# A ring of value tiles in another part of memory, eighteen stores on another queue, and a new order for the first of two phases

## The chip, the core and the metric

The kernel runs on one core of a Trainium2 chip. Five engines work side by side: TensorE (PE; the loads of its stationary operand are shown apart as PEld), VectorE (DVE), ScalarE (ACT), GpSimd (POOL) and SyncE (SP), which here does nothing but issue transfers (DMAs) between the chip's DRAM and the on-chip SBUF. [...] The metric is the device time of one execution in microseconds (us), taken as the median of several runs.

## What is computed

A decoder layer in float32 over 32 batches of 128 rows of 512 values: causal self-attention with rotary positions, cross-attention to a context, and a feed-forward block with ternary weights. A residual and a layer norm follow each. Cut to what matters:

```python
def self_attention(x):                      # x [32, 128, 512], 16 heads of 32
    q, k, v = heads(x @ Wq.T), heads(x @ Wk.T), heads(x @ Wv.T)
    q, k = rope(q), rope(k)
    s = where(causal, q @ k.T / sqrt(32), -inf)
    return merge(softmax(s) @ v) @ Wo.T

def cross_attention(x, ctx):                # 8 heads of 16: a head is 16 of the 128 ROWS
    q, k, v = (t.reshape(32, 8, 16, 512) for t in (x, ctx, ctx))
    s = einsum('bhdq,bhdl->bhql', q, k) / sqrt(16)      # 512 x 512 for each head
    return gamma * einsum('bhql,bhdl->bhdq', softmax(s), v).reshape(32, 128, 512)

def bitlinear(x, w, b):                     # int8 activations, weights of -1, 0 and 1
    return act_quant(rms_norm(x)) @ weight_quant(w).T + b

def ffn(x):                                 # 512 -> 2048 -> 512
    h = gelu(silu(bitlinear(x, w1, b1)))
    return bitlinear(layer_norm(h, g, b), w2, b2)

x = ln(x + self_attention(x))
x = ln(x + cross_attention(x, ctx))
out = ln(x + ffn(x))
```

## The kernel before

**Two phases.** Phase 1 (L255 to L591) does the self-attention of all 32 batches and leaves its results in DRAM. Phase 2 (L594 to the end) does cross-attention and the feed-forward block of all 32 batches from there. The *seam* below is the stretch in which the last batches of phase 1 (batch 31 is the last) and the first of phase 2 meet.

**Phase 1, a batch.** `load` fetches x as it is and transposed. `project` (L338 to L348) multiplies by a weight of 512 columns. Both operands are split into a high and a low part, which gives 12 matmuls of 128x512 in three steps of four; a step is one unit for the planner. A batch has four projections: queries and keys (*side* 0 and 1 of `rope`), values, and the output projection `wo`. `rope` turns queries and keys by products on DVE (L407 to L410) and sums on POOL (L414, L415). `stage_s` transposes both (L430, tile `banka`, copied by DVE to `qkT`) and computes the scores of 16 heads in four groups that the code calls heads 0 to 3 (L447). The softmax of a group goes mask and row maximum on DVE (L459), exponential on ACT (L465), reciprocal and product on DVE or POOL, four transposes on PE (L477) and a copy (L480, tile `prT`). `stage_o` weighs the values (L496), projects, and normalises on POOL (L514 to L519) into `x1`, which is stored in DRAM as `x1d` (L521).

**The parts.** `split3` (L350 to L365) turns a float32 tile into three bfloat16 parts: a cast on ACT, a difference on POOL (tile `spr`), a cast on ACT, a difference on POOL. All three lie in a tile `sp`. Six DMAs of 128 KB then store parts 0, 1, 2, 0, 1, 0 one after the other as `qd` (L364). `context` does the same with the context: six stores as `kd`, with the parts in another order, and the values times gamma as `cd`. With 96 rows of such parts (six pairs of 16 rows) one bfloat16 matmul of phase 2 gives nearly a float32 product. `quantize_weights` prepares the ternary weights in between.

**Phase 2, half a batch (four heads).** `kp` and `qp` are tiles of 98 rows x 4 heads x 512: 96 rows of parts, and two rows that shift the scores by their maximum. In `kp` these are ones (from the DRAM tile `ones_d`), in `qp` the negated maxima, in a high and a low part (tiles `mhi`, `mlo`). The work goes: 16 times scores `mx` on PE (L677) and a maximum on DVE (L681); a transpose, and two rows of maxima (L694, L695) stored into `qp` by two SP DMAs (L700); then 16 scores `sT` on PE with all 98 rows (L756), 16 exponentials `ex` on ACT (L759) and 16 matmuls with the values, `acc` (L766). The values lie in a ring of three tiles `cT` of 128 x 32 x 32 float32: half of each tile is loaded from `cd` (L663), the other half is ones, set once (L616), so that the same matmul gives the sum of the exponentials. Softmax division, layer norm and feed-forward block follow.

**Who sets the order.** Nothing is written down in the order in which it runs. `Plan` (L83 to L217) is a list scheduler that runs while the program is built. Every operation has a kind ("PE.qkv", "SP.xs"), a cost in us, and a priority: its batch number plus the offset of its kind in a table, `OFF1` for phase 1 and `OFF2` for phase 2. At each step the planner takes, among the first open operation of every kind, the one that can start in the earliest time slot, and in one slot the one of lowest priority. Each engine then runs its instructions in exactly the planned order, and so a changed offset or cost reorders engines and queues and nothing else. A DMA is one operation of "SP" with a cost for its issue and a latency until it has landed.

**The seam in the code.** When the last projection of queries, keys and values ("PE.qkv") has been planned, the planner calls `early` (L578). It releases the projection weights, which lie at the right end of SBUF, and opens a pool "qk" there with four `kp` and four `qp` tiles. Twelve SP DMAs fill them for the first two batches of phase 2: for each tile pair a ones row, the key parts, the query parts. These twelve stand in the middle of SP's queue, among the stores of the last batches of phase 1. The tiles of phase 2 proper, the `cT` ring among them, come from pools opened after phase 1 on the left, where phase 1's working tiles were. So the three memsets of L616 are the first that POOL does in phase 2.

```python
        pl.op("SP." + kind, max(0.55, kb / 340), fn, ins, outs, prio, 2.2 + kb / 340, rel)
        ...
        st2.close()
        qk = pool(ctx, "qk", side="right")
        ...
    vring = [cb.tile([P, 2 * XD, NC * XH], F32, tag=f"cT{i}", name=f"cT{i}") for i in range(CFG["cT"])]
    for t in vring:
        nc.gpsimd.memset(t[:, XD:], 1.0)
```

The framework adds the waits between engines: one of a tile's later user for an earlier one, one of a newly opened pool's tile for those that used the same place, and one for each DMA completion that is needed. A DMA's completion is counted on one of a few semaphores that all DMAs of the program use in turn.

Of the kernel before, what the change touches and what calls it, by code (L numbers as in the profile page):

```python
# [11 lines left out]
F32 = mybir.dt.float32  # L12
# [11 lines left out]
P = 128  # L24
# [5 lines left out]
XH = 8  # L30
XD = S // XH
DI = 2048
NC = D // P
# [9 lines left out]
Q_PARTS = (0, 1, 2, 0, 1, 0)  # L43
# [23 lines left out]
OFF1 = {'SP.x': 76.47, 'SP.w': -83.56, 'ACT.w': 1251.46, 'DVE.wl': 97.39, 'DVE.w': 1455.82, 'SP.wq': 258.11, 'ACT.wq': -501.07, 'DVE.wq': -718.11, 'PE.wq': 497.75, 'ACT.xh': -83.03, 'Pool.xl': -493.52, 'PE.qkv': 642.06, 'DVE.rope': -749.29, 'Pool.rope': 726.68, 'ACT.v': -277.88, 'SP.cx': 161.38, 'ACT.cs': 561.27, 'Pool.cs': 151.36, 'Pool.cs3': 444.12, 'SP.cs': -169.59, 'SP.ct': -341.75, 'ACT.ct': 5.76, 'SP.cv': 657.35, 'PE.qkT': -233.53, 'DVE.qkT': -713.26, 'PE.sc': 223.31, 'DVE.mask': -673.03, 'ACT.exp': 343.93, 'DVE.rd': 481.16, 'DVE.pr': 893.48, 'PE.prT': -342.18, 'DVE.prT': 602.51, 'ACT.prT': 121.56, 'Pool.pr': 38.32, 'PE.pv': 403.29, 'ACT.oh': 297.53, 'DVE.ol': -241.16, 'PE.wo': 645.28, 'DVE.y': -873.41, 'Pool.y': 255.11, 'Pool.x1': -113.85, 'SP.x1': 730.76, 'ACT.xs': 299.8, 'Pool.xs': -1039.81, 'Pool.xs3': 582.54, 'SP.xs': 975.4}  # L67
C1 = dict(pace=15.0, xs=4, pr=5, prT=7, ra=3, qkT=4, sp=3, spr=2, xhe='ACT', lne='Pool', s1e='Pool', s2e='ACT', cxl=-0.5, wq=3.0, nb=32, wst=4, mm=3, tr=3, sc=4, scc=1.1, po=1, pc=4, spe='ACT', cte='ACT', s3e='Pool', qke='DVE', pre=['DVE', 'DVE', 'Pool', 'Pool'], prTe=['DVE', 'ACT', 'ACT', 'ACT'], wl=24.0, slack=0.02)

class Buf:  # L70

# [11 lines left out]
class Plan:  # L83
# [5 lines left out]
    slack = 0.1  # L89
# [131 lines left out]
def decoder_kernel(ctx: ExitStack, tc: tile.TileContext, x, xT, cx, cxT, wqkT, wvT, woT, gamma,  # L221
                   w1T, b1, ln_g, ln_b, w2T, b2, cst, out):
    nc = tc.nc

    def pool(stack, name, bufs=1, **kw):
        return stack.enter_context(tc.tile_pool(name=name, bufs=bufs, **kw))
# [23 lines left out]
    q_d = [dram.tile([6, XD, XH, D], BF16, tag=f"qd{b}", name=f"qd{b}") for b in range(NB)]  # L250
# [4 lines left out]
    with ExitStack() as st1:  # L255
# [6 lines left out]
        pl = Plan(nc, tc, OFF1)  # L262
        NB1 = C1['nb']

# [33 lines left out]
        def dma(kind, fn, kb, ins=(), outs=(), prio=0.0, rel=0.0):  # L298
            pl.op("SP." + kind, max(0.55, kb / 340), fn, ins, outs, prio, 2.2 + kb / 340, rel)
# [38 lines left out]
        def project(kind, pq, parts, w, sl, wb, prio):  # L338

            steps = [(a, t, c) for a, t in ((0, 0), (1, 0), (0, 1)) for c in range(NC)]  # L340
            m = C1['pc']
            for i in range(0, 12, m):
                def mm(i=i):
                    for k in range(i, i + m):
                        a, t, c = steps[k]
                        nc.tensor.matmul(pq.t, parts[a].t[:, c, :], w[t][:, c, sl], start=k == 0, stop=k == 11)  # L346
                used = [parts[0]] + ([parts[1]] if i + m > 4 else [])
                pl.op("PE." + kind, 0.236 * m, mm, used + [wb], (pq,), prio)  # L348

        def split3(kind, v, dst, parts, prio):  # L350

            sp, r = pl.buf("sp"), pl.buf("spr")
            e = C1['spe']
            pl.op(f"{e}.{kind}", 0.48 if e == "ACT" else 0.6, lambda: cp(e)(sp.t[:, 0, :], v.t), (v,), (sp,), prio)

            e1, e2 = C1['s1e'], C1['s2e']
            pl.op(f"{e1}.{kind}", 0.6 if e1 == "DVE" else 1.225, lambda: en(e1).tensor_tensor(
                r.t, v.t, sp.t[:, 0, :], ALU.subtract), (v, sp), (r,), prio)
            pl.op(f"{e2}.{kind}", 0.52 if e2 == "ACT" else 0.34, lambda: cp(e2)(sp.t[:, 1, :], r.t), (r,), (sp,), prio)  # L359
            e3 = C1['s3e']  # L360
            pl.op(f"{e3}.{kind}3", 1.0 if e3 == "DVE" else 1.2, lambda: en(e3).tensor_tensor(  # L361
                sp.t[:, 2, :], r.t, sp.t[:, 1, :], ALU.subtract), (r, sp), (sp,), prio)
            for s, k in enumerate(parts):
                dma(kind, lambda s=s, k=k: nc.sync.dma_start(dst[s].rearrange("t h c -> h t c"), sp.t[:, k, :]), 131,  # L364
                    (sp,), (), prio)  # L365

        def context(b):
            at = b
# [117 lines left out]
        def stage_o(b):  # L486
            at = b
            po, oh, ol, v = pl.buf("po"), pl.buf("oh"), pl.buf("ol"), PV[b]
# [30 lines left out]
            pl.op(e + ".x1", 0.46 if e == "DVE" else 0.76, lambda: en(e).tensor_scalar(  # L519
                x1.t, y.t, nm.t, rs.t, ALU.add, ALU.mult), (y, nm, rs), (x1,), at)  # L520
            dma("x1", lambda: nc.sync.dma_start(x1_d[b], x1.t), 262, (x1,), (), at)  # L521
            split3("xs", x1, q_d[b], Q_PARTS, at)


        def quantize_weights(k, src, dst):
# [47 lines left out]
            stage_o(b)  # L573
        pl.slack = C1['slack']
        NQ = CFG['NQ']
        kring, qring = [], []

        def early():  # L578

            st2.close()  # L580
            qk = pool(ctx, "qk", side="right")
            for i in range(NQ):
                k = qk.tile([NROW, 4, D], BF16, tag=f"kp{i}", name=f"kp{i}")
                q = qk.tile([NROW, 4, D], BF16, tag=f"qp{i}", name=f"qp{i}")
# [22 lines left out]
    for name, n, shape, dtype in (  # L607
# [2 lines left out]
            ("q1T", 2, (P, NC, P), FP16), ("z", CFG["z"], (P, DI), F32), ("q2", 2, (P, DI), FP16),  # L610
            ("q2T", CFG["q2T"], (P, NI, P), FP16), ("t1", 1, (P, D), F32)):
        pl.tag(name, n, pb, shape, dtype)

    vring = [cb.tile([P, 2 * XD, NC * XH], F32, tag=f"cT{i}", name=f"cT{i}") for i in range(CFG["cT"])]
    for t in vring:
        nc.gpsimd.memset(t[:, XD:], 1.0)  # L616
    pl.tag("cT", CFG["cT"], ring=vring)
    pl.tag("kp", NQ, ring=kring)
    pl.tag("qp", NQ, ring=qring)
# [465 lines left out]
```

## Time and profile before

| what | value |
|---|---|
| runs | 1667.03, 1671.82 and 1674.67 us; median 1671.82 |
| the profiled execution | 1675.28 us; span 1673.5 us, granted TensorE clock 0.973 |
| PE, PEld | 1551.4 us (93%), 785.0 us (47%) |
| DVE, ACT, POOL | 1383.9 us (83%), 1432.7 us (86%), 1251.5 us (75%) |
| DMA queue of the kernel | 256.78 MB, 52.8% of 16 engines' span |
| DRAM | 142.41 MB read, 92.81 MB written |
| 0 to 50 us | PE busy 33.46, ACT 22.72 |
| 600 to 700 us | PE busy 95.31 |
| 800 to 1000 us | PE 193.23, DVE 185.27, ACT 187.33, POOL 170.47 |
| 1400 to 1600 us | PE 186.23 |
| 1600 us to the end | PE 27.65 |

All times inside an execution are counted from the start of its span; the 1.8 us between span and time lie around it. Phase 1 runs until about 565 us and phase 2 from there. The costliest lines, from the groups of instructions (line, engine, operation, output tile and input tile, shapes, count; busy us and mean ns of one; idle time before them and what ended most of it):

```profile
L681 DVE TENSOR_REDUCE mt<-mx 128x1 f32<-128x512 f32 x1024 | 643.4, 679 | 54.9 <-PE mx L677 52.9
L759 ACT ACTIVATE ex<-sT 128x512 f32<-128x512 f32 x1024 | 533.9, 615 | 77.9 <-PE sT L756 74.4
L677 PE MATMUL mx<-kp,qp 96*128 96x512 bf16 x1024 | 336.9, 386 | 21.5 <-DVE mt L681 17.7
L756 PE MATMUL sT<-qp,kp 98*128 98x512 bf16 x1024 | 320.7, 385 | 15.9 <-DMA qp<-mlo 13.3
L766 PE MATMUL acc<-ex,cT 128*32 128x512 f32 x2048 | 289.4, 637 | 0.0
```

A wait is shown as the name behind "<-": the instruction or DMA whose end released the one that stood idle. A queue of SP is written "SPq", and a DMA "DMA qd<-sp" by the tiles it goes from and to.

### The profile page before, as it was taken

How to read it: one execution, taken by the hardware profiler on the slowest of the kernel's cores; microseconds unless marked ns; L12 is line 12 of the kernel's file. 1: busy time of each engine (PE TensorE's matmuls, PEld its weight loads, DVE VectorE, ACT ScalarE, POOL GpSimd, SP SyncE). 2: the span in 40 equal slices, each digit the busy share in tenths (PEclk: the TensorE clock that was granted, in tenths of full speed). 3: DMA queues.
4: the chain of work that ended last, by engine and by line, in shares of the span. 5: the costliest groups of instructions: out<-in, count | busy, mean ns of one | idle time of the engine just before them, and what ended most of it. 6: DMA issues, size and time to landing. Idle time of an engine off the chain costs nothing.

```text
span 1673.5 us, 30270 instructions
## 1 busy us (share of the span) xinstructions
PE 1551.4 (93%) x9540; PEld 785.0 (47%) x9540; DVE 1383.9 (83%) x3315; ACT 1432.7 (86%) x2950; POOL 1251.5 (75%) x1679
## 2 busy tenths in 40 slices
PE   6999999999999799999999999999999999999844
PEld 4878777777778333333333333333333333333211
DVE  6877776777777678899999989899899999998674
ACT  4889989899976367999989989899999999998963
POOL 3777778777787404679879888878978888986772
PEclk8999999999999799999999999999999999999977
DMA  6476677766664654355455345545544544544221
GB/s 226 163 236 232 226 231 244 255 233 214 209 208 153 185 177 122 93 129 145 113 133 147 105 129 139 131 115 139 142 110 128 153 110 134 149 122 123 69 62 50
DMA packets 235680, 258.71 MB, mean 155 GB/s; under 512 B 110072, under 2 KB 159224, under 8 KB 235136
## 3 DMA queue, kind: packets, MB, share of 16 engines
q1 hardware_dynamic: 235520, 256.78, 52.8%
q8 instruction: 75, 1.23, 0.3%
q14 instruction: 85, 0.70, 0.1%
HBM read 142.41 MB, written 92.81 MB: 141 GB/s over the span
## 4 chain that ended last, share of the span: by engine, by line
PE 41%; DVE 18%; POOL 16%; DMA 9%; ACT 8%; issue 7%; SPq 1%; POOLq 0%; ACTq 0%; DVEq 0%
PE banka L346 12%; DVE mt L681 8%; PE acc L766 7%; PE sT L756 6%; POOL z L972 6%; PE mx L677 5%; PE m L925 2%; DVE am L998 2%; PE banka L477 2%; DMA qd<-sp 2%; POOL z L794 2%; PE banka L447 2%; ACT pr L465 1%; ACT ex L759 1%; PE banka L496 1%
## 5 line engine op out<-in xcount | busy, mean ns | idle before, releaser
L681 DVE TENSOR_REDUCE mt<-mx 128x1 f32<-128x512 f32 x1024 | 643.4, 679 | 54.9 <-PE mx L677 52.9
L759 ACT ACTIVATE ex<-sT 128x512 f32<-128x512 f32 x1024 | 533.9, 615 | 77.9 <-PE sT L756 74.4
L677 PE MATMUL mx<-kp,qp 96*128 96x512 bf16 x1024 | 336.9, 386 | 21.5 <-DVE mt L681 17.7
L756 PE MATMUL sT<-qp,kp 98*128 98x512 bf16 x1024 | 320.7, 385 | 15.9 <-DMA qp<-mlo 13.3
L766 PE MATMUL acc<-ex,cT 128*32 128x512 f32 x2048 | 289.4, 637 | 0.0
L465 ACT ACTIVATE pr<-pr,nm 128x128 f32<-128x128 f32 x512 | 198.9, 394 | 4.1 <-DVE nm L459 4.1
L756 PEld LDWEIGHTS <-kp 98*128 98x128 bf16 x1024 | 90.3, 98 | 223.7 <-issue 125.1
L677 PEld LDWEIGHTS <-qp 96*128 96x128 bf16 x1024 | 96.3, 98 | 195.5 <-issue 95.1
L972 POOL TENSOR_TENSOR z<-z,bb_b 128x512 f32<-128x512 f32 x119 | 154.4, 1301 | 0.3
L972 POOL TENSOR_TENSOR z<-z,g_b 128x512 f32<-128x512 f32 x119 | 153.5, 1297 | 0.5
L459 DVE CUSTOM_DVE_ANT_0 pr<-banka,cmask 128x128 f32<-128x128 f32 x512 | 111.0, 286 | 35.9 <-PE banka L447 35.2
L1009 PE MATMUL m<-w2q,q2T 128*128 128x512 fp8e4 x464 | 116.7, 385 | 16.4 <-DMA q2T<-q 16.4
L766 PEld LDWEIGHTS acc<-ex,cT 128*32 128x32 f32 x2048 | 70.6, 184 | 114.1 <-issue 108.8
L925 PE MATMUL m<-w1q,q1T 128*128 128x512 fp8e4 x464 | 119.1, 378 | 2.7 <-DVE z L928 1.3
L1009 PEld LDWEIGHTS <-q2T 128*128 128x128 f16 x512 | 51.0, 101 | 104.5 <-DMA q2T<-q 34.9
L465 ACT ACTIVATION_READ_ACCUMULATOR pr<-pr,nm 128x1 f32 x512 | 98.0, 191 | 0.0
L794 POOL TENSOR_SCALAR z<-z,nmu,rs 128x512 f32<-128x512 f32 x119 | 94.5, 801 | 1.8
L361 POOL TENSOR_TENSOR sp<-spr,sp 128x512 bf16<-128x512 f32 x64 | 76.7, 1200 | 20.3 <-ACT sp L359 18.2
L928 DVE SCALAR_TENSOR_TENSOR z<-m,dq,b_b 128x512 f32<-128x512 f32 x116 | 85.0, 733 | 1.8 <-PE m L925 1.5
L925 PEld LDWEIGHTS <-q1T 128*128 128x128 f16 x512 | 49.2, 97 | 76.1 <-issue 19.9
L846 POOL TENSOR_TENSOR num<-num,rden 128x512 f32<-128x512 f32 x29 | 37.1, 1278 | 62.3 <-DMA rden<-rd 62.2
L346 PE MATMUL banka<-wqkh,xh 128*128 128x512 f32 x256 | 73.9, 411 | 10.3 <-ACT xh L388 10.3
(152 smaller groups left out, 3247.9 us busy)
## 6 DMA issues: line engine op xcount, KB each, us to landing
kd<-sp SPq DMA_DIRECT2D x192, 128.0 KB
qd<-sp SPq DMA_DIRECT2D x192, 128.0 KB
kp<-kd SPq DMA_DIRECT2D x64, 384.0 KB
qp<-qd SPq DMA_DIRECT2D x64, 384.0 KB
F<-f SPq DMA_DIRECT2D x64, 256.0 KB
xt<-in_xT SPq DMA_DIRECT2D x32, 256.0 KB
xs<-in_x SPq DMA_DIRECT2D x32, 256.0 KB
ct<-in_cxT SPq DMA_DIRECT2D x32, 256.0 KB
```

The costliest lines, as they stand in the source:

```text
L346: nc.tensor.matmul(pq.t, parts[a].t[:, c, :], w[t][:, c, sl], start=k == 0, stop=k == 11)
L459: nc.vector.tensor_tensor_reduce(pr.t[:, c, :], sc.t[:, c * P:(c + 1) * P], cmask, -1.0, 3e38, ALU.add, ALU.min, nm.t[:, c:c + 1])
L465: nc.scalar.activation(pr.t[:, c, :], pr.t[:, c, :], AF.Exp, scale=-1.0, bias=nm.t[:, c:c + 1], accum_out=den.t[:, c:c + 1])
L677: nc.tensor.matmul(sc.t[:, j, :], q.t[0:NPR, h, (qc + j) * P:(qc + j + 1) * P], k.t[0:NPR, h, :], start=True, stop=True)
L681: pl.op("DVE.mx", 0.064 + 0.534 * W, lambda: nc.vector.tensor_reduce(mt.t[:, i:i + W], sc.t, AX.X, ALU.max), (sc,), (mt,), p, join=True)
L756: nc.tensor.matmul(sc.t[:, i, :], k.t[:, h, lc * P:(lc + 1) * P], q.t[:, h, :], start=True, stop=True)
L759: pl.op("ACT.ex", 0.052 + 0.426 * SW, lambda: nc.scalar.activation(ex.t[:, j:j + SW, :], sc.t, AF.Exp, scale=1.0 / XD ** 0.5), (sc,), (ex, ...
L766: nc.tensor.matmul(acc.t[32 * h:32 * h + 32, :], v.t[:, :, XH * lc + 4 * g + h], exs[h // 2].t[:, h % 2, :], start=lc == 0, stop=lc == NC - 1)
L794: pl.op(e + "." + p, cost + 0.1, lambda: en(e).tensor_scalar(o.t[:, sl], v.t[:, sl], sh.t, sc.t, ALU.add, ALU.mult), ins, outs, prio)
L925: nc.tensor.matmul(flat(pz)[:, i * 512:(i + 1) * 512], q1T.t[:, c, :], w1q[:, c, (n + i) * 512:(n + i + 1) * 512], start=c == 0, stop=c == ...
L972: pl.op(e + kind, 0.148 + 0.0021 * w if e == "Pool" else 0.05 + 0.00105 * w, lambda: en(e).tensor_tensor(t(), t(), other[:, sl], op), src, ...
L1009: nc.tensor.matmul(flat(py)[:, 0:D], q2T.t[:, c, :], w2q[:, c, :], start=c == 0, stop=c == NI - 1)
```

## The change

Five edits, all of them around phase 1 and the seam. Phase 2's table `OFF2`, its settings and its code stay as they are, but for the place of the ring.

1. The table `OFF1` has new offsets for all kinds of phase 1, and one new kind, "ACT.xsd".
2. The planner's cost of a projection matmul is 0.244 us instead of 0.236.
3. `split3` has a parameter `late`. For the last three batches (29, 30 and 31) it is true for the query parts: their 18 stores are issued by ScalarE (`nc.scalar`), with a kind of their own, a cost of 0.55 and a latency of 2.6. All other stores stay on SyncE.
4. The three `cT` tiles come from the pool "qk" at the right end, ahead of the `kp` and `qp` tiles, where projection weights were.
5. Their memsets are issued in `early`, that is, in POOL's queue in the middle of phase 1's last batches, and no longer at the start of phase 2.

```diff
-OFF1 = {'SP.x': 76.47, 'SP.w': -83.56, 'ACT.w': 1251.46, ...
+OFF1 = {'SP.x': 69.66, 'SP.w': -164.57, 'ACT.w': 1533.56, ... 'ACT.xsd': 300.57}
-C1 = dict(pace=15.0, xs=4, ...
+C1 = dict(late=3, pace=15.0, xs=4, ...
...
-                pl.op("PE." + kind, 0.236 * m, mm, used + [wb], (pq,), prio)
+                pl.op("PE." + kind, 0.244 * m, mm, used + [wb], (pq,), prio)
...
-        def split3(kind, v, dst, parts, prio):
+        def split3(kind, v, dst, parts, prio, late=False):
...
             for s, k in enumerate(parts):
-                dma(kind, lambda s=s, k=k: nc.sync.dma_start(dst[s].rearrange("t h c -> h t c"), sp.t[:, k, :]), 131,
-                    (sp,), (), prio)
+                q = nc.scalar if late else nc.sync
+                pl.op("ACT.xsd" if late else "SP." + kind, 0.55, lambda s=s, k=k, q=q: q.dma_start(
+                    dst[s].rearrange("t h c -> h t c"), sp.t[:, k, :]), (sp,), (), prio, 2.6)
...
-            split3("xs", x1, q_d[b], Q_PARTS, at)
+            split3("xs", x1, q_d[b], Q_PARTS, at, b >= NB1 - C1['late'])
...
-        kring, qring = [], []
+        kring, qring, vring = [], [], []
         def early():
             st2.close()
             qk = pool(ctx, "qk", side="right")
+            for i in range(CFG["cT"]):
+                t = qk.tile([P, 2 * XD, NC * XH], F32, tag=f"cT{i}", name=f"cT{i}")
+                nc.gpsimd.memset(t[:, XD:], 1.0)
+                vring.append(t)
             for i in range(NQ):
...
-    vring = [cb.tile([P, 2 * XD, NC * XH], F32, tag=f"cT{i}", name=f"cT{i}") for i in range(CFG["cT"])]
-    for t in vring:
-        nc.gpsimd.memset(t[:, XD:], 1.0)
     pl.tag("cT", CFG["cT"], ring=vring)
```

The stores that remain on SyncE have a planned cost of 0.55 and a latency of 2.6 as well; `dma` gives 0.55 and 2.2 + 131 / 340 = 2.59 for them before.

More of the change, by code (lines that the diff above doesn't have):

```diff
@@ L66 @@
 OFF2 = {'SP.const': -264.67, 'x.kq': 390.3, 'SP.v': 77.29, 'PE.mx': -381.13, 'DVE.mx': 126.92, 'PE.mT': -632.22, 'DVE.mT': 8.23, 'SP.m': -156.28, 'PE.sT': -531.43, 'ACT.ex': -687.83, 'PE.pv': 37.38, 'ACT.acc': -737.17, 'SP.f': 49.63, 'SP.fd': 1119.71, 'SP.fn': 725.19, 'SP.fx': 343.0, 'DVE.rd': -172.57, 'SP.fr': -316.31, 'SP.fb': 17.98, 'Pool.y': -355.28, 'DVE.y': -82.99, 'Pool.yn': -277.59, 'DVE.c1': -57.25, 'Pool.c1': -358.01, 'Pool.c1m': -627.03, 'Pool.q1a': -78.8, 'Pool.x2b': 72.59, 'SP.q1T': -375.73, 'PE.c1': 39.79, 'DVE.z': -137.9, 'ACT.gelu': -406.78, 'DVE.nmu': -80.22, 'ACT.sq': -333.32, 'Pool.zn': -48.07, 'Pool.zt': 303.63, 'Pool.zb': -221.61, 'ACT.sq2': 252.58, 'DVE.am2': 91.79, 'Pool.c2': -682.87, 'Pool.c2m': -291.19, 'ACT.q2a': -262.61, 'DVE.q2a': -514.12, 'SP.q2T': 382.04, 'PE.c2': 86.97, 'DVE.c3': 17.23, 'Pool.c3': -278.83, 'Pool.c3n': 302.38, 'SP.out': 77.71, 'SP.kq': -42.69, 'DVE.yn': -735.62, 'DVE.c1m': 785.24, 'DVE.q1a': 467.22, 'DVE.zn': 550.15, 'DVE.zb': -508.13, 'DVE.c2m': -306.12, 'DVE.c3n': 99.96}
-OFF1 = {'SP.x': 76.47, 'SP.w': -83.56, 'ACT.w': 1251.46, 'DVE.wl': 97.39, 'DVE.w': 1455.82, 'SP.wq': 258.11, 'ACT.wq': -501.07, 'DVE.wq': -718.11, 'PE.wq': 497.75, 'ACT.xh': -83.03, 'Pool.xl': -493.52, 'PE.qkv': 642.06, 'DVE.rope': -749.29, 'Pool.rope': 726.68, 'ACT.v': -277.88, 'SP.cx': 161.38, 'ACT.cs': 561.27, 'Pool.cs': 151.36, 'Pool.cs3': 444.12, 'SP.cs': -169.59, 'SP.ct': -341.75, 'ACT.ct': 5.76, 'SP.cv': 657.35, 'PE.qkT': -233.53, 'DVE.qkT': -713.26, 'PE.sc': 223.31, 'DVE.mask': -673.03, 'ACT.exp': 343.93, 'DVE.rd': 481.16, 'DVE.pr': 893.48, 'PE.prT': -342.18, 'DVE.prT': 602.51, 'ACT.prT': 121.56, 'Pool.pr': 38.32, 'PE.pv': 403.29, 'ACT.oh': 297.53, 'DVE.ol': -241.16, 'PE.wo': 645.28, 'DVE.y': -873.41, 'Pool.y': 255.11, 'Pool.x1': -113.85, 'SP.x1': 730.76, 'ACT.xs': 299.8, 'Pool.xs': -1039.81, 'Pool.xs3': 582.54, 'SP.xs': 975.4}
@@ L68 @@
-C1 = dict(pace=15.0, xs=4, pr=5, prT=7, ra=3, qkT=4, sp=3, spr=2, xhe='ACT', lne='Pool', s1e='Pool', s2e='ACT', cxl=-0.5, wq=3.0, nb=32, wst=4, mm=3, tr=3, sc=4, scc=1.1, po=1, pc=4, spe='ACT', cte='ACT', s3e='Pool', qke='DVE', pre=['DVE', 'DVE', 'Pool', 'Pool'], prTe=['DVE', 'ACT', 'ACT', 'ACT'], wl=24.0, slack=0.02)
+OFF1 = {'SP.x': 69.66, 'SP.w': -164.57, 'ACT.w': 1533.56, 'DVE.wl': 224.13, 'DVE.w': 1487.99, 'SP.wq': 296.08, 'ACT.wq': -463.09, 'DVE.wq': -742.95, 'PE.wq': 461.12, 'ACT.xh': -34.87, 'Pool.xl': -579.88, 'PE.qkv': 642.47, 'DVE.rope': -636.7, 'Pool.rope': 753.46, 'ACT.v': -325.1, 'SP.cx': 56.25, 'ACT.cs': 587.4, 'Pool.cs': 196.32, 'Pool.cs3': 467.79, 'SP.cs': -292.4, 'SP.ct': -402.26, 'ACT.ct': 97.5, 'SP.cv': 685.21, 'PE.qkT': -268.05, 'DVE.qkT': -750.98, 'PE.sc': 176.14, 'DVE.mask': -511.77, 'ACT.exp': 361.28, 'DVE.rd': 495.43, 'DVE.pr': 1021.3, 'PE.prT': -437.64, 'DVE.prT': 623.36, 'ACT.prT': 100.45, 'Pool.pr': 84.22, 'PE.pv': 437.14, 'ACT.oh': 229.14, 'DVE.ol': -202.02, 'PE.wo': 645.76, 'DVE.y': -849.92, 'Pool.y': 94.83, 'Pool.x1': -7.25, 'SP.x1': 682.13, 'ACT.xs': 266.21, 'Pool.xs': -957.67, 'Pool.xs3': 476.1, 'SP.xs': 1037.25, 'ACT.xsd': 300.57}
@@ L70 @@
+C1 = dict(late=3, pace=15.0, xs=4, pr=5, prT=7, ra=3, qkT=4, sp=3, spr=2, xhe='ACT', lne='Pool', s1e='Pool', s2e='ACT', cxl=-0.5, wq=3.0, nb=32, wst=4, mm=3, tr=3, sc=4, scc=1.1, po=1, pc=4, spe='ACT', cte='ACT', s3e='Pool', qke='DVE', pre=['DVE', 'DVE', 'Pool', 'Pool'], prTe=['DVE', 'ACT', 'ACT', 'ACT'], wl=24.0, slack=0.02)
 class Buf:
```

## The prediction, made before the changed kernel was run

> **What bounds the kernel now.** I read the table by windows first, then the chain of waits around the seam between the phases, then the order in time there. The first shows who is busy in each stage (columns: stretch, its length, busy time of PE, PEld, DVE, ACT and POOL with counts, granted TensorE clock, DMA share, GB/s):
>
> ```profile
> 50.00:548.00 498.00, 488.20 (x4064) 391.45 (x4061) 366.24 (x1554) 440.38 (x1419) 381.25 (x441) 1.00 0.66 219
> 548.00:565.00 17.00, 14.14 (x93) 10.30 (x92) 10.33 (x26) 11.09 (x37) 12.49 (x17) 1.00 0.86 231
> 565.00:586.00 21.00, 12.99 (x25) 2.21 (x24) 14.61 (x26) 1.24 (x2) 5.42 (x9) 0.52 0.54 184
> 586.00:600.00 14.00, 14.00 (x69) 4.59 (x68) 9.10 (x16) 9.65 (x19) 0.00 (x0) 0.87 0.22 64
> ```
>
> Phase 1 is TensorE's: from 50 to 548 us it idles 498.00 - 488.20 = 9.8 us, so a new plan of the same work has little to win there. The seam is not TensorE's: between 565 and 586 PE is busy 13 of 21 us, at a clock of 0.52. What holds it is a chain of DMAs (start, length, what):
>
> ```profile
> 550.96 7.67 DMA qp<-qd
> ...
> 558.69 6.67 DMA qd<-sp
> ...
> 565.44 4.83 DMA qd<-sp
> ...
> 571.42 5.36 DMA x1d<-x
> ...
> 576.79 5.44 DMA qd<-sp
> ...
> 582.45 1.45 POOL cT L616 x3
> ```
>
> The last query-part store is issued at 576.79 and lands at 582.23. The value ring's memset waits for it, and so does the SyncE queue:
>
> ```profile
> 563.31 1.27 SPq L521 DMA_DIRECT2D x1d<-x  x2
> ...
> 568.86 0.77 POOL L519 TENSOR_SCALAR x<-ya,nm,rs 128x512 f32<-128x512 f32 x1 [2.81 <-DMA x1d<-x]
> ...
> 572.05 5.31 SPq L364 DMA_DIRECT2D qd<-sp  x8
> ...
> 582.37 0.33 SPq L663 DMA_DIRECT2D cT<-cd  x1
> 582.75 0.62 SPq L700 DMA_DIRECT2D qp<-mhi  x1
> 583.42 0.57 SPq L700 DMA_DIRECT2D qp<-mlo  x1
> ...
> 585.55 1.44 PE L756 MATMUL sT<-qp,kp 98*128 98x512 bf16 x3 [7.06 <-DMA qp<-mlo]
> ...
> 586.22 1.58 ACT L759 ACTIVATE ex<-sT 128x512 f32<-128x512 f32 x3 [14.06 <-PE sT L756]
> ```
>
> The value load stands in SyncE's queue with every store before it as its wait; the two row maxima (mhi, mlo), which DVE has finished by 574.87, stand behind it until 582.75. So the first exponential of phase 2 comes at 586.22. The order of every engine in phase 2 is the same in both built programs, and PE is busy 193 to 197 of every 200 us there, so what the first exponential gains or loses should reach the end.
>
> **The start of phase 1.** PE idles 3.06 us before the first transposes (15.78 to 18.84) and 2.64 us for the last value weight (24.54 to 27.18). The new order puts a 1.7 us step of the second projection into the first gap, and batch 0's second transposes ahead of the value projection. Walking it with the old rows: second projection ends at 22.9, its rotation 3.06 us later (25.96), transposes 0.4, value steps held by the same weight at 27.18, scores, last value step: 33.4 against 33.81. I take -0.4, between -3.1 (the whole gap saved) and +2 (a step of 1.9 us in front of late data).
>
> **The rest of phase 1.** The PE work is the same, instruction for instruction in number. What changes is how much of it stands between a batch's scores and the transposes of its fourth head, that is, what covers the softmax: counted in order at 0.93 us per four wide matmuls, 0.44 per four transposes, 1.10 per scores and 1.01 per weighing, 13.94 us in the mean before, 13.29 after, the least 10.2 in both. In 50 to 548 us PE waited 16 times behind the softmax, 8.5 us together, 3.2 of them so:
>
> ```profile
> PE banka L496 <- ACT prT L480: 3.2, 4, 1.8
> ```
>
> If each such wait grows by 0.65: +10.4; if all vanish: -8.5. I take +1, the middle, because nearly all heads have 12 us of cover on both sides.
>
> **The memset, moved into POOL's queue of phase 1.** Three of 0.52 us, 1.45 together, now stand behind the last projection (549.12) and before POOL's step on batch 28 (548.91). That step starts at 550.6 instead of 548.91; ACT's cast behind it stalls from 550.85 to 551.77, and the last two heads' exponentials, the last weighing and all of the tail with them: +1.0. The old place (582.45) held nobody, since the first matmul that reads cT is at 590.06: saved there, 0.
>
> **The 18 stores on ACT.** Each DMA of the program counts on one of eight semaphores, and its issue waits until the DMA before it on that semaphore has landed. By the built program's waits, the ones row of kp3 on SyncE now waits for the second store of batch 29, which ACT issues; the kp3 and qp3 loads for the third and fourth; four of batch 28's six stores for later ones of batches 29 and 30; x1d29 for the kp3 load; and batch 31's normalisation on POOL for x1d29, as before. So SyncE stands at 552 until ACT gets to its stores. Step by step, 0.58 per issue (the median of the row of these stores on SyncE, 576 ns; there is no DMA issue on ACT in this trace):
> - ACT's cast before the stores ends at 561.05 + 1.0 = 562.05; the second store starts at 562.65 and lands after 3.0, between 2.1 (the mlo row, 583.42 to 585.52, on quiet engines) and 6.67: 565.65. The old SyncE passed this place at 552.99.
> - kp3 load at 566.3, qp3 at 567.5, the six stores of batch 28 to 571.4. x1d29 needs the kp3 load: 3.5 us (the load of 549.46, landed by 552.99) to 7.67; I take 5.0: 571.4. It lands 5.5 later (563.31 to 568.86 before): 577, between 575 and 579.5.
> - Batch 31 on POOL then starts 8.1 us later than its 568.86. From there: 0.77, cast 0.62, three stores 1.74 (POOL's 1.15 beside them), cast 0.62, six more stores 3.5: the last issue starts 7.2 later (7.93 before), at 584.2.
> - It lands 4.4 later (3.0 to 5.44): 588.6, between 585 and 592.
>
> The first exponential waits for all these stores in both programs, since its pool is released as a whole: before it was free at 582.23 and the maxima came later; now the maxima come first (x1d31 at 577.8, landed 583.2, mlo behind it on its semaphore, 585.3) and the stores decide. 588.6 - 586.22 = +2.4. PE has done three score matmuls and two maxima matmuls by then; its fourth, at 587.64 before, follows the first exponential at 589.2: +1.6, between -2 and +5.
>
> Here the Trainium skill speaks against the change. The seam's share of 0.54 at 184 GB/s, with 1.00 and 332 GB/s in 600 to 605 us, leaves room for a second issuer. "DMA: Bandwidth & Descriptors", section Issuing engines are not separate DMA queues, says that issuing from more engines saves only the issuer's own time. By it the gain is at most 18 x 0.58 = 10.4 us of SyncE's queue; by the row the landing is what waits, and the sum goes by that.
>
> **The sum.** -0.4 + 1 + 1.6 (the memset is inside it) = +2.2. The profiled execution took 1675.28 us for a span of 1673.5, so 1677.5; the median of the runs, 1671.82, is 3.46 below that execution: 1674.0.
>
> **Rivals.**
> - *The seam does what it was rebuilt for.* If ACT's stores land so early that x1d29 isn't held, the last store is issued near 576 and lands near 580: 580.2 instead of 586.22, -6, with -0.4 and half of phase 1's softmax waits (-4): 1661. For it: the idle ACT (1.24 us in 565 to 586). Against: the kp3 row's wait, which a faster DMA can't move ahead of ACT's cast.
> - *An issue costs more on ACT.* Price: two stores before the kp3 row, two more before x1d29's chain, ten after batch 31 is ready, so 14 issues in line. At SyncE's slowest, 1.24 us, 14 x 0.66 = 9.2 more: 1683. It makes the kernel slower by 0.5% from 1.02 us per issue.
> - *The thinner cover bites:* +10.4 instead of +1: 1683. For it: ACT is 440 of 498 us busy. Against: the least cover is unchanged.
> - *The change does not do what it says:* the stores move but gain nothing, SyncE isn't held either, and the last store lands at 582.2 plus the memset's 1.0: the maxima no longer matter, 583.3, -3: 1668.
>
> **How the numbers follow.** The forecast has 0.52, the rivals 0.17, 0.13, 0.13 and 0.05. 0.5% is 8.4 us, about what a measurement of this kernel can tell from no change. Forecast: 0.05 faster, 0.40 the same, 0.07 slower; first rival 0.13 faster, 0.04 the same; second 0.09 slower, 0.04 the same; third 0.11 slower, 0.02 the same; last 0.02 faster, 0.02 the same, 0.01 slower. Together 0.20, 0.52, 0.28. The three terms' bounds, taken as independent, give 1674 - 10.4 and + 11.5: range 1664 to 1685, which takes in the slower rivals and leaves out most of the first.
>
> **What would show it.** Right: in the profile after, the kp<-ones_d row that was at 552.99 stands near 565; x1d<-x for batch 29 near 571; the first exponential is released by a store, within 3 us of 588.6; the last projection ends within 3 us of 549.1 and POOL's memset follows it at once. Wrong: if SyncE's queue flows through 553 to 563 as before, if ACT's issues are longer than 0.8 us, or if PE's idle time in 50 to 548 is more than 5 us off 9.8.

## The result and the profile after

The changed kernel takes 1686.52 us (median of 6 runs, 1683.19 to 1689.70), the kernel before 1670.75 us in 6 runs beside it. The ratio is 1.0071 with a 95% interval of 1.0052 to 1.0090: slower by 0.7%, some 12 us. (The two medians lie further apart, 15.8 us, but the six runs of the kernel before alone spread over 10 us; the ratio with its interval is used from here on.) The profiled execution took 1683.79 us for a span of 1682.0 us, 8.5 us longer than that before.

**Where the time goes.** First the table by windows, in the stretches shown of before (columns as there):

```profile
50.00:548.00 498.00, 482.43 (x3923) 382.35 (x3922) 355.97 (x1494) 431.76 (x1393) 368.88 (x433) 1.00 0.67 217
548.00:565.00 17.00, 16.48 (x169) 13.04 (x167) 13.86 (x52) 12.09 (x47) 10.34 (x17) 1.00 0.42 111
565.00:586.00 21.00, 16.58 (x75) 6.21 (x75) 15.39 (x28) 4.22 (x8) 9.55 (x14) 0.81 0.61 183
586.00:600.00 14.00, 4.95 (x11) 1.21 (x10) 5.00 (x9) 2.02 (x4) 3.08 (x3) 0.50 0.49 160
```

PE did 3923 matmuls in 498 us where it did 4064, and from 548 to 565 it is still at work that was over before. So phase 1 itself is longer, and the whole seam is moved back. Fixed windows can't say by how much, since the work in them differs. Equal work can. Each matmul that the trace records in phase 1 gets its usual length (0.2335 us in a projection, 0.11 in a transpose, 0.0345 in the scores and 0.0316 in the weighing, which have 32 records each in a batch); that makes 512 us. The *middle* below is the stretch from the moment 40 us of this work are done to the moment 480 are: the same 440 us of PE work in every kernel. The table by windows, with just this stretch, before and then after:

```profile
65.16:527.90 462.74, 452.94 (x3715) 362.49 (x3714) 336.52 (x1410) 413.59 (x1319) 357.77 (x416) 1.00 0.68 226
```

```profile
63.24:536.69 473.45, 458.08 (x3716) 362.95 (x3714) 335.46 (x1402) 409.30 (x1310) 350.76 (x413) 1.00 0.67 219
```

The counts agree to one matmul, and the second takes 10.7 us more at the same clock. Half of it is idle time; the other half looks like 5.1 us more busy time, because the ends of matmuls are modelled and a short wait hides in them. The waits of PE in this stretch (who waits for whom; us in total, times, longest), three before and then the same three after:

```profile
PE banka L430 <- POOL ra L415: 1.1, 3, 0.5
PE banka L496 <- ACT prT L480: 3.2, 4, 1.8
PE banka L477 <- POOL pr L470: 1.1, 4, 0.4
```

```profile
PE banka L431 <- POOL ra L416: 5.0, 7, 2.0
PE banka L497 <- ACT prT L481: 4.8, 4, 1.8
PE banka L478 <- POOL pr L471: 3.2, 7, 1.3
```

The second and third are the softmax: the weighing and the transposes of the probabilities. The first is the transposes of queries and keys, which wait for the rotation on POOL. Where the hidden half went shows when matmuls are counted from start to start: what is above their usual lengths is 22.9 us before and 33.6 after. Ahead of the weighing it grew by 5.2 us (3.7 to 8.9), ahead of the transposes of queries and keys by 4.8 (2.4 to 7.2), ahead of those of the probabilities by 0.7 (9.5 to 10.2); the rest is 7.3 us in both.

**The seam after**, in order of time:

```profile
570.99 2.52 ACTq L365 DMA_DIRECT2D qd<-sp  x3
...
574.96 0.23 SPq L593 DMA_DIRECT2D kp<-ones_d  x1
...
577.37 6.47 SPq L365 DMA_DIRECT2D qd<-sp  x6
...
583.94 0.89 SPq L522 DMA_DIRECT2D x1d<-x  x2
...
588.03 0.77 POOL L520 TENSOR_SCALAR x<-ya,nm,rs 128x512 f32<-128x512 f32 x1 [10.79 <-DMA x1d<-x]
588.83 0.32 SPq L522 DMA_DIRECT2D x1d<-x  x1
588.84 0.62 ACT L354 CAST sp<-x 128x512 bf16<-128x512 f32 x1 [14.67 <-POOL x L520]
...
590.76 4.91 ACTq L365 DMA_DIRECT2D qd<-sp  x7
...
599.22 1.09 ACT L761 ACTIVATE ex<-sT 128x512 f32<-128x512 f32 x2 [7.86 <-DMA qd<-sp]
```

The waits of SyncE's queue from 540 to 600 have this line, and before the change no such line:

```profile
SPq L593 <- DMA qd<-sp: 8.3, 1, 8.3
```

This is the chain of the prediction, link for link: the ones row of the fourth key tile (L593) waits 8.3 us for a store and stands at 574.96. In the trace it counts on the same semaphore as ScalarE's second store, issued at 572.24. SyncE's stores and the x1 stores come behind it, POOL's step on batch 31 waits 10.79 us for one of them, ACT 14.67 us for POOL, and the first exponential is released by a store. The last projection of queries, keys and values ended at 558.2 here and at 549.1 before; from there to the first exponential it takes 41.0 us and took 37.1.

### The profile page after: what moved, and what is told of

It is laid out like the page before. It is cut to its first block, busy times and chain, and to the rows that moved or that the text cites. A ratio compares the mean times of both kernels' runs of the same rounds, so it can differ in the third digit from the quotient of the medians.

```text
span 1682.0 us, 30248 instructions
## 1 busy us (share of the span) xinstructions
PE 1554.0 (92%) x9540; PEld 783.9 (47%) x9540; DVE 1386.0 (82%) x3315; ACT 1431.0 (85%) x2950; POOL 1245.9 (74%) x1679
## 4 chain that ended last, share of the span: by engine, by line
PE 37%; POOL 18%; DVE 14%; ACT 12%; DMA 9%; issue 4%; SPq 2%; ACTq 0%; POOLq 0%; DVEq 0%
PE banka L346 9%; PE acc L768 7%; DVE mt L683 6%; POOL z L974 6%; PE sT L758 6%; PE mx L679 5%; ACT pr L466 4%; PE m L927 2%; DVE am L1000 2%; PE banka L478 2%; POOL z L796 2%; DMA rden<-rd 1%; ACT ex L761 1%; DMA den<-F 1%; PE banka L448 1%
## 5 line engine op out<-in xcount | busy, mean ns | idle before, releaser
L1011 PE MATMUL m<-w2q,q2T 128*128 128x512 fp8e4 x464 | 117.6, 387 | 16.5 <-DMA q2T<-q 16.5
L848 POOL TENSOR_TENSOR num<-num,rden 128x512 f32<-128x512 f32 x29 | 37.9, 1308 | 68.2 <-DMA cT<-cd 53.2
L361 POOL TENSOR_TENSOR sp<-spr,sp 128x512 bf16<-128x512 f32 x64 | 75.8, 1188 | 14.8 <-ACT sp L359 13.9
L390 POOL TENSOR_TENSOR xl<-xt,xh 128x512 fp32r<-128x512 f32 x32 | 42.5, 1327 | 59.3 <-ACT xh L389 59.3
```

The source lines that it names most:

```text
L1011: nc.tensor.matmul(flat(py)[:, 0:D], q2T.t[:, c, :], w2q[:, c, :], start=c == 0, stop=c == NI - 1)
```

## The experiments

All kernels compute the whole of it, and nothing is left out in any. Each ratio is to runs of the kernel before that were taken beside it. The same numbers were read off every trace. *Projection* is the end of the last projection of queries, keys and values, *PE end* that of the last matmul of phase 1, *exponential* the start of the first one of phase 2, *seam* the time from projection to exponential; all in us of one profiled execution.

| kernel | ratio to before (95%) | middle | projection | PE end | exponential | seam |
|---|---|---|---|---|---|---|
| before | 1 | 462.7 | 549.1 | 562.6 | 586.2 | 37.1 |
| after | 1.0071 (1.0052 to 1.0090) | 473.5 | 558.2 | 572.7 | 599.2 | 41.0 |
| e1, plan alone | 1.0041 (1.0020 to 1.0062) | 471.5 | 555.7 | 569.2 | 593.6 | 37.9 |
| e2, ring and stores, old plan | 1.0041 (1.0024 to 1.0058) | 462.1 | 545.2 | 559.7 | 585.4 | 40.2 |
| e3, ring alone | 0.9983 (0.9962 to 1.0003) | 462.5 | 544.3 | 558.9 | 579.8 | 35.5 |
| e4, stores alone | 1.0035 (1.0017 to 1.0053) | 465.7 | 551.0 | 564.5 | 593.4 | 42.4 |
| e5, cost 0.244 alone | 1.0061 (1.0036 to 1.0086) | 471.3 | 554.4 | 570.5 | 595.6 | 41.2 |
| e6, new PE order, rest by the old table | 1.0194 (1.0162 to 1.0227) | 495.0 | 583.1 | 596.6 | 619.6 | 36.5 |
| e7, old PE order, rest by the new table | 1.0197 (1.0166 to 1.0229) | 493.3 | 578.4 | 591.9 | 615.3 | 36.9 |
| e8, ring, stores of 30 and 31 | 1.0036 (1.0017 to 1.0054) | 461.8 | 547.8 | 562.3 | 588.6 | 40.8 |
| e9, ring, stores of 31 | 1.0004 (0.9986 to 1.0022) | 463.9 | 548.2 | 562.7 | 583.9 | 35.7 |
| e10, offsets alone | 1.0060 (1.0041 to 1.0079) | 464.4 | 544.8 | 568.2 | 593.3 | 48.4 |
| e11, cost 0.228 alone | 1.0092 (1.0071 to 1.0112) | 458.2 | 544.3 | 573.4 | 604.8 | 60.5 |
| e12, ring, 0.228 then 0.236 | 1.0076 (1.0051 to 1.0101) | 457.5 | 540.8 | 566.5 | 597.2 | 56.4 |

How far one execution can be trusted: six kernels have the old order of phase 1 (before, e2, e3, e4, e8, e9). Their middles lie within 461.8 and 465.7, 463.1 in the mean, but their projections end anywhere from 544.3 to 551.0, in part because the moment at which the first 40 us of work are done already differs by 4.5 us. So the middle of one execution can be compared to some 4 us, and ends can't. The seam depends on the plan as well (e1 and e5 move neither ring nor stores and have 37.9 and 41.2), so it is compared here between kernels of one plan; and as each was profiled once, a difference of 1 or 2 us in it is a hint and no more.

### Plan or seam

**e1, the plan alone.** The kernel before with the table and the cost of the changed one:

```diff
-OFF1 = {'SP.x': 76.47, 'SP.w': -83.56, ...
+OFF1 = {'SP.x': 69.66, 'SP.w': -164.57, ... 'ACT.xsd': 300.57}
-                pl.op("PE." + kind, 0.236 * m, ...
+                pl.op("PE." + kind, 0.244 * m, ...
```

> The kernel before with the new offsets of phase 1 and the projection matmul's cost of 0.244, nothing else: no store on ScalarE, the ring in its old place. TensorE and VectorE run in the order of the changed kernel. Theory 'plan': the 9.1 us by which the last projection ends later in the changed kernel (558.2 against 549.1) come from the new order of phase 1, so the last projection ends at 557 to 559 here too, TensorE's stalls ahead of the weighing, the transposes of the probabilities and those of queries and keys grow by 4.8, 2.1 and 4.9 us, and the time is 8 to 11 us above the kernel before. Rival 'seam': the new order costs +1 as forecast, and what delays phase 1 is the ring's place or the stores on ScalarE: the last projection ends within 2 us of 549, and the time is within 3 us of the kernel before.

Measured +0.41%. The middle takes 471.5 us, 8.4 above the mean of the old order, and the same two waits lead in the trace:

```profile
PE banka L430 <- POOL ra L415: 4.3, 6, 1.4
PE banka L496 <- ACT prT L480: 3.6, 5, 1.3
```

No store and no ring was moved in this kernel, so the loss of phase 1 belongs to the plan. The last projection ends at 555.7, a little before the 557 to 559 expected, and the time, 6.9 us, is a little under the 8 expected.

**e2, the seam alone.** The changed kernel with `OFF1` and the cost of before.

> The changed kernel with the old offsets and the old cost of 0.236: ring moved, 18 stores on ScalarE, old order of phase 1. Theory 'plan': the last projection ends near 549.1 again, and from there to the first exponential of phase 2 it takes 41 us as in the changed kernel (37.1 before), so the first exponential comes at 590 and the time is +3 to +5. Rival 'seam': +8 to +12, with the last projection late. Rival 'they belong together' (the seam was arranged for the new plan and only loses under it): the first exponential comes before 586 and the time is -2 to -6.

Measured +0.41%, +6.9 us of 1677.5. The middle is that of the old order, the seam takes 40.2 us. "They belong together" falls: with the old plan the seam loses as with the new. (The first exponential does come before 586, at 585.4, but only because the last projection ends at 545.2 in this execution.) The time is above the 3 to 5 us expected, though its interval reaches down to 4.0, and above the 3.1 us by which the seam is longer; the rest isn't explained by the trace of one execution. The two halves add up: 1.0041 times 1.0041 is 1.0082, and the changed kernel has 1.0071.

**e3 and e4, the two halves of the seam.** Old plan; in e3 `late=0`, so that only the ring and its memsets move; in e4 the stores move and the ring stays on the left.

> The kernel before with the value ring and its memsets moved alone; all stores on SyncE, old order. Theory 'plan': the value load and the two rows of maxima no longer wait for the last store, so the first exponential waits for that store alone: 582.2, with up to 1.0 for the memset in GpSimd's queue, and an exponential follows at 583 to 584 instead of 586.2: -2 to -3 us. Rival: the memset in GpSimd's queue is worth more than it saves: the first exponential at 587 to 588, +1 to +2.

> The kernel before with the 18 stores on ScalarE alone; the ring in its old place, old order. Theory 'plan': SyncE's ones row of the fourth key tile waits for the second store of batch 29, batch 29's x1 store behind it, batch 31's normalisation behind that; the last store lands near 590, and then the value load and the two rows of maxima come one after the other as before: the first exponential near 593, +6 to +8 us. Rival 'stores help': the last store lands before 582 and the first exponential comes before 586, -1 to -6.

The ring alone shortens the seam to 35.5 us and gives a ratio of 0.9983, whose interval reaches 1.0003: a gain of 1.6 us in the trace that the times don't clear of nothing. The stores alone lengthen the seam to 42.4 us and cost 0.35%. So the loss of the seam is the stores'. By the traces the ring pays a part of it back (42.4 us without it, 40.2 with it), because the value load, and the row maxima behind it, no longer wait until the last store has landed; the times don't show this, with 1.0035 for the stores alone and 1.0041 for both.

### What of the plan, what of the stores

**e5, the cost alone.** One number: `0.236 * m` becomes `0.244 * m`, old offsets.

> The kernel before with the planner's cost of a projection matmul at 0.244 instead of 0.236, old offsets, nothing else. Four such matmuls take 0.934 us in the trace (0.2335 each), so 0.944 was planned before and 0.976 with 0.244. Theory 'overstated cover': a planner that takes a projection for longer than it is puts less of it ahead of the transposes that wait for the softmax; counted in the built programs the work between the scores and the fourth head's transposes is 13.93 us before, 13.40 here and 13.29 in the changed kernel. So most of the loss of phase 1 is here: the stretch between the 40th and the 480th us of TensorE's phase 1 work, 463 us in the four profiles with the old order and 472 in the two with the new, takes 467 to 473, and the time is +4 to +9. Rival 'the offsets': the cost alone is worth nothing, that stretch takes 461 to 465, and the time is within 3 us of the kernel before.

Measured +0.61%, 10.2 us, where 4 to 9 were expected; middle 471.3 us. The cost alone brings the whole longer middle. The seam is longer too, 41.2 us, though no store and no ring was moved.

**e6 and e7, the order of one engine.** The planner may take a PE operation only if it is the next in a recorded order; the other engines are planned afresh around it. e6 holds PE to the new order with the old table and cost, e7 to the old order with the new ones:

```diff
+                if fixed and k in KINDS and k != fixed[0]:
+                    continue
                 o = self.kinds[k][i]
...
+            if fixed and o.kind == fixed[0]:
+                fixed.pop(0)
             o.fn()
```

> The kernel before in which TensorE's order of phase 1 is held to that of the new plan, word for word, and all other engines are planned by the old offsets and the old cost around it. Theory 'TensorE's order': the loss comes along, 470 to 474 us for the stretch of 440 us of TensorE's work (463 before, 472 with the new plan), stalls ahead of the transposes of queries and keys and ahead of the weighing some 9 us above those before, time +6 to +10. Rival 'the others' order' (GpSimd's rotation sums come late because of where they stand in GpSimd's queue, the shorter cover is not needed): 461 to 466 us, time within 3 us of the kernel before.

> The reverse: new offsets and a cost of 0.244 for all engines, with TensorE's order of phase 1 held to that of the kernel before. Theory 'TensorE's order': 461 to 466 us for the stretch, time within 3 us of the kernel before. Rival 'the others' order': 469 to 474 us, +6 to +10.

Both miss. Each mixture is slower by almost 2%, with a middle of 495.0 and 493.3 us; in e7, with PE in the order of the fast kernel, PE waits for the rotation eleven times (L444 here is L430 before):

```profile
PE banka L444 <- POOL ra L429: 17.5, 11, 3.8
```

But these aren't the old plan with one engine exchanged. PE runs in the recorded order and VectorE nearly in the order that goes with it, while the others got a third order. In e6 an instruction of ScalarE stands 8.4 places in the mean from its place before and 7.1 from its place in the changed kernel, which are 4.7 apart; for GpSimd it is 3.3 and 4.3 against 2.1, for SyncE's DMAs 8.1 and 9.9 against 6.9, and e7 is further off still. So what is shown is that a plan made around a foreign order of PE loses 2%; which engine's order carries the loss of the changed kernel stays open.

**e8, stores of two batches.** e2 with `late=2`.

> Old plan, ring moved, and the stores on ScalarE for the last two batches alone (30 and 31). Counted in the built program, the ones row of the fourth key tile then waits for the load of the third key tile, not for a store of batch 29 that ScalarE issues. Theory 'shared semaphore': SyncE's queue flows again (the ones row within 6 us of the one before it, where it took 14.4 in the changed kernel), GpSimd's step on batch 31 isn't held, and from the last projection to the first exponential it takes 32 to 34 us (37.1 before, 35.5 with the ring alone, 40.2 with all 18 stores and the old plan): -3 to -5 us. Rival 'stores from ScalarE are late by themselves' (they stand behind its casts and take longer to land): 38 to 41 us, +1 to +4.

The seam takes 40.8 us: the rival's number. But its reason isn't the rival's. SyncE stands still as before, now for another store (the waits of SyncE's queue from 540 to 600; who waits for what, us in total, times, longest):

```profile
SPq L595 <- DMA qd<-sp: 6.6, 2, 5.7
```

L595 loads the key and query parts, and the 5.7 us are those of the fourth key tile. The built program has this load wait for batch 30's first store on ScalarE, and in the trace both count on one semaphore (the store issued at 562.34, the load at 565.06). The expectation had looked at the ones row alone, and that one came 5.1 us after the DMA before it, as expected. The semaphores are handed out in the order that the framework makes of all DMAs, so when batch 29's stores went back to SyncE, batch 30's took their place beside the loads.

### The last batch, and which part of the plan

**e9, stores of one batch.** e2 with `late=1`.

> Old plan, ring moved, stores on ScalarE for batch 31 alone. Counted in the built program no load of SyncE waits for a store that ScalarE issues (the fourth key tile's ones row waits for the first key load, as before); in the run with two batches its load waited for batch 30's first store, 5.7 us. Theory 'shared semaphore': SyncE's ones row comes within 6 us of the one before it, GpSimd's step on batch 31 starts within 21 us of the last projection as before (568.86 - 549.12 = 19.7), and the first exponential comes 31 to 34 us after the last projection (35.5 with the ring alone, 37.1 before, 40.8 with two batches, 40.2 with three): -3 to -6 us. Rival 'stores from ScalarE are late by themselves': 37 or more, no gain over the kernel before.

SyncE's loads flow: the fourth ones row comes at 552.85, 1.6 us after the DMA before it, and POOL's step on batch 31 starts 20.4 us after the projection. Yet the seam takes 35.7 us, not 31 to 34 and no less than with the ring alone, and the time shows no gain over the kernel before. The order in time tells why:

```profile
573.98 0.33 SPq L522 DMA_DIRECT2D x1d<-x  x1
577.36 1.22 SPq L365 DMA_DIRECT2D qd<-sp  x2
578.63 0.60 SPq L665 DMA_DIRECT2D cT<-cd  x1
579.33 0.73 SPq L702 DMA_DIRECT2D qp<-mhi  x1
580.16 0.56 SPq L702 DMA_DIRECT2D qp<-mlo  x1
...
583.92 1.57 ACT L761 ACTIVATE ex<-sT 128x512 f32<-128x512 f32 x3 [11.93 <-PE sT L758]
```

The stores no longer come last. The row of maxima does (DVE has it from 574.98), and it stands in SyncE's queue behind two stores of batch 30 that begin 3.0 us after the x1 store's issue has ended: by the built program the fifth store of batch 30 on SyncE waits for the second of batch 31 on ScalarE, and in the trace they count on one semaphore (issued at 577.36 and 572.77). The same coupling, at a third place.

**e10, the offsets alone**, cost 0.236. **e11, the cost as far below**: `0.228 * m`, old offsets.

> The kernel before with the new offsets of phase 1 and the old cost of 0.236. Theory 'overstated cover': the cost carries the loss, the work between scores and the fourth head's transposes is 13.63 us in the mean (13.93 before, 13.40 with the new cost alone), so the stretch of 440 us of TensorE's work takes 462 to 467 us and the time is 0 to +4. Theory 'fitted order' (any disturbance of a plan whose engines were fitted to each other loses, whatever its covers): 468 us or more, +5 or more.

> The kernel before with a cost of 0.228 instead of 0.236, as far below as the changed kernel's is above; old offsets. The work between scores and the fourth head's transposes grows to 14.54 us in the mean (13.93 before, 13.29 in the changed kernel), that between a projection and its transposes to 4.84 (4.42, 4.33). Theory 'overstated cover': TensorE stalls less, the stretch takes 455 to 462 us (463 before), the time is 0 to -6. Theory 'fitted order': 468 us or more, +5 or more, though the covers are longer.

Each theory is right about one half. The middle goes with the cover: 464.4 us with the offsets alone, and with the low cost 458.2, 4.9 us *shorter* than the mean of the old order. But both kernels are slower, by 0.60% and 0.92%, as "fitted order" said, and lose it behind the middle: PE ends 23.4 and 29.1 us after the projection instead of 13.5. This loss has a place that neither theory named. In the kernel before, all 192 stores of context parts (`kd`) are issued by 516.8, long before the last projection ends, and in every kernel with a seam of 42.4 us or less none is issued after it. In e10 12 of them are, in e11 24: these plans leave the context of the last two or four batches until the projections are through.

### Keep the middle, keep the end

**e12.** Ring moved; `(0.228 if prio < 26 else 0.236) * m`, so that the last six batches are planned by the old cost.

> The kernel before with the ring moved (as in the run with the ring alone) and with the planner's cost of a projection matmul at 0.228 for batches below 26 and 0.236 from there; all stores on SyncE, old offsets. Counted in the built program the work between the scores and the fourth head's transposes is 14.48 us in the mean and 10.2 at least (13.93 and 10.2 before, 14.54 and 9.3 with 0.228 throughout), and TensorE's work behind the weighing of batches 28 to 31 is 42.4, 18.2, 13.5 and 2.8 us, nearly that before (44.3, 18.7, 13.5, 2.8; with 0.228 throughout 26.5, 21.4, 12.5, 2.8). If the cover sets the middle of phase 1 and the order of the last batches its end: the stretch of 440 us of TensorE's work takes 456 to 460 us (463 before, 458 with 0.228 throughout), the last projection of phase 1's outputs ends 13 to 15 us after the last projection of queries, keys and values, the first exponential comes 35 to 37 us after that projection, and the time is -4 to -8 us below the kernel before. If every disturbance of the order loses: +5 or more.

The middle is the shortest of all, 457.5 us, and the time is 0.76% above before: the end was missed again. The waits of e12 from 520 to 570, PE and then ACT, name one wait:

```profile
PE banka L346 <- ACT oh L500: 11.5, 1, 11.5
```

```profile
ACT sp L354 <- DMA kd<-sp: 10.9, 1, 10.9
```

ACT's cast of a batch into `sp` (three buffers) waits 10.9 us for a store of context parts, and PE waits behind ACT. In e11 ACT waits 12.1 us for such a store, and PE 11.8 us behind ACT. In e12 too 24 stores of context parts are issued after the last projection, from 548.55 on: SyncE's queue first stands 4.4 us until the projection has ended, then issues the twelve loads of the seam, and these stores come behind them. So the old cost for the last six batches brought back, by the count of the expectation, PE's work behind the last weighings, but not the contexts. That late contexts go with a long end is seen in e10, e11 and e12; no run moved the contexts alone. Which plan keeps the shorter middle and early contexts was not tried; no kernel here is clearly faster than before.

## Why the prediction went wrong where it did

The sum had the change slower by 2.2 us, with no change as the likeliest case; the kernel became slower by 0.7%, 11.9 us, which had 0.28. The sign of the sum was right and its size a fifth of what came. The ratio, set against the 1671.82 us of the runs shown, gives 1683.7, near the upper end of the range of 1664 to 1685; the median itself, 1686.5, is 1.5 above it. That 1683.7 lies in the range is owed to the wide bounds, not to the sum: both main terms came out near or above their upper bounds. (Taken as independent, as the text says, the bounds give -10.5 and +10.3, so the range would end at 1684 and not at 1685.) Of the signs of being wrong one came: PE's idle time from 50 to 548 us is 15.6 us, 5.8 off 9.8. And of those of being right one failed clearly: the last projection ended 9.1 us late.

**"The rest of phase 1", +1: the step that failed.** It measured +8.4 (e1) to +10.4 (after) against the old order's 463.1 us. Two things were wrong in it. First, the value between the ends, -8.5 and +10.4, was taken in the middle "because nearly all heads have 12 us of cover"; what PE lost behind the softmax grew by 5.9 us (5.2 ahead of the weighing, 0.7 ahead of the transposes), six times the +1. PE waits in a few places, 4 to 7 times for each of the main waits, and 12 us of cover did not keep it from waiting there. Nor does the cover of a batch tell where: by the count of the table below, among batches 2 to 28 of the changed kernel those that lose 1 us or more behind the softmax have a cover of 13.9 us in the mean, the others 14.2. Second, the cover counted was that of the softmax alone. The transposes of queries and keys, which wait for POOL's rotation, lost 4.8 us more (the visible wait went from 1.1 to 5.0) and were in no term. The third rival has the number, +10.4, but in part by luck: its reason, the softmax, accounts for 5.9 of it.

**The cost of 0.244 had no term at all.** The trace gives 0.2335 per matmul. With the higher cost the planner holds the same projections for a longer cover and puts fewer of them ahead of a transpose. The work between the scores and the fourth head's transposes stands beside the middle in six orders. It is counted with the full length of scores and weighing; the prediction names these lengths too, but its 13.94 and 13.29, and the counts of the expectations, come out with half of them:

| order | mean cover, us | middle, us |
|---|---|---|
| new plan (after, e1) | 13.82 | 472.5 |
| e5, 0.244 alone | 13.96 | 471.3 |
| e10, offsets alone | 14.35 | 464.4 |
| old plan (six kernels) | 14.56 | 463.1 |
| e12, 0.228 then 0.236 | 15.24 | 457.5 |
| e11, 0.228 | 15.29 | 458.2 |

That the cost alone makes the middle longer is shown (e5), and that the middle falls as the cover grows is seen in these six orders, up to 0.7 us between the last two. That the cover is the cause, and not something else that the planner moves with it, is not shown. The two runs meant to isolate it don't: e6 and e7 have the new and the old order of PE, and so its covers, and middles of 495.0 and 493.3 us, because the other engines' orders changed as well.

**The start, -0.4.** Not to be seen: the first 40 us of work end between 60.7 and 65.2 us whatever the order, and within the old order alone they scatter as widely.

**The memset, +1.0.** Right in place and size. It stood where forecast, 558.27 to 559.72 right behind the last projection, and phase 1 ends 14.5 us after that projection in all five kernels with the moved ring and the old or new plan whole (after, e2, e3, e8, e9), 13.5 in the three with the ring on the left (before, e1, e4). With the ring's gain behind it the seam was still 1.6 us shorter (e3). The prediction had priced the gain of the ring at nothing, since the old memset's place "held nobody"; what gained was the value load, which no longer kept the maxima waiting for the last store.

**The 18 stores, +2.4 to the first exponential.** Right in mechanism, too small in size. After the last projection, forecast and measured: the ones row 16.5 and 16.8 us, the x1 store of batch 29 22.3 and 25.7, the last issue 35.1 and 36.9, the first exponential 39.5 and 41.0. The seam grew by 3.9 us, with the old plan by 3.1, and in the times the seam alone cost 6.9 us (e2, 4.0 to 9.7) where the sum had +1.6. (The sum let it reach the end because PE is busy 193 to 197 of every 200 us in phase 2; the windows have 186 to 197.) An issue on ACT takes 588 ns in the median where 0.58 us was taken from SyncE's rows. So the second rival, which asked for 1.24 us per issue, falls; the first, a seam that gains, falls with e2, and the last, stores that change nothing, with e4. e8 and e9 show the coupling through shared semaphores moving with the batches.

The page "DMA: Bandwidth & Descriptors" of the Trainium skill, section Issuing engines are not separate DMA queues, says that starting DMAs from several engines only saves the sequencer's time for the start. The runs agree: with the ring moved, one batch's stores on ScalarE leave the seam at 35.7 us against 35.5. The runs have a price beside it: in e4, e8 and e9 one queue stands still for the other.

## What to carry to other kernels

Before DMAs are moved to another queue, read in the built program which DMA each later one waits for: where completions share a few semaphores, a queue stops for transfers that it never issued. A planner's cost is a promise of cover: raising that of a projection from 0.236 to 0.244, where 0.2335 was measured, cost 0.6%. But the plan had been tuned as a whole, and every change to it here, up, down or mixed, lost 0.4 to 2%. Compare two orders by equal work, and the middle apart from the end: a middle 5 us shorter (e11, e12) came with a seam 19 to 23 us longer. And when a run is to exchange the order of one engine, compare the orders of the others before reading its time.

## What the hardware showed besides

In phase 2, from 600 to 1560 us, the granted clock of PE drops to half for single stretches of 3.4 or 6.8 us. The order of its matmuls there is the same in all fourteen kernels, and the drops come at few places of it: in the fourteen profiles 27 of 28 begin near the 287th, 587th, 2095th or 2480th matmul recorded in phase 2. One execution has none to four of them (none in the changed kernel's and in e6's, four in e2's). The kernel before has three, and in the 3.4 us ahead of each PE is busy for 2.2, 1.8 and 1.8 us. Why one execution drops at a place and the next does not, isn't shown. Before, the long stretch and one drop:

```profile
605.00:1563.00 958.00, 926.22 (x4829) 328.53 (x4822) 883.31 (x1502) 879.54 (x1337) 761.39 (x1087) 0.99 0.49 128
699.00:706.00 7.00, 6.82 (x21) 1.80 (x20) 4.14 (x8) 6.28 (x11) 0.87 (x3) 0.52 0.22 56
```

In the changed kernel's profiled execution there is none in this stretch:

```profile
605.00:1563.00 958.00, 927.14 (x4866) 329.87 (x4865) 887.49 (x1508) 882.67 (x1349) 757.52 (x1080) 1.00 0.49 131
```

It does 37 more matmuls in the same 958 us. At the 200th matmul of phase 2 the changed kernel was 13.7 us late (635.5 against 621.8); by 1340 us it was 4.0 us late, and 6.2 of the 9.7 us went within the three drops of the other execution's clock (2.9, 1.7 and 1.6); at the end of the span it was 8.5. So two single spans say little about a loss of this size, and the ratio of many runs, 0.71%, is the number to go by.
